# Performer features in two row halves of the array, two chunks of tokens at a time

## The chip, the cores and the metric

The program runs on one core of one Trainium2 chip. The metric is device time in microseconds (us), the median of several executions; one more execution is recorded by the hardware profiler. The engines are named as in the profile: PE is TensorE (matrix products), PEld its weight loads, DVE is VectorE, ACT is ScalarE, POOL is GpSimd, SP is SyncE.

## The reference

The model is a stack of four layers on an input of 8 images of 128 channels and 16 x 16 pixels (256 tokens an image, 2048 in all). Layer 0 is an "adder" convolution (sums of absolute differences), layer 1 a Mamba block, layer 2 attention and a mixture of experts, layer 3 a Performer with eight inner layers and a spectral filter at the end. The change is in the attention of the Performer: each head of 16 dimensions turns its keys and queries into 44 positive features.

```python
B, W, D, H, DEP, LAT = (8, 8192, 128, 8, 4, 10)
DH = D // H          # 16
M = 44
def softmax_kernel(data, proj, is_query, eps=0.0001):
    dn = data.shape[-1] ** (-0.25)
    ratio = proj.shape[0] ** (-0.5)
    dd = jnp.einsum('bhnd,md->bhnm', data * dn, proj)
    diag = jnp.sum(data * data, axis=-1, keepdims=True) * 0.5 * (dn * dn)
    if is_query:
        mx = jnp.max(dd, axis=-1, keepdims=True)
    else:
        mx = jnp.max(dd, axis=(-1, -2), keepdims=True)
    return ratio * (jnp.exp(dd - diag - mx) + eps)
...
    qp = softmax_kernel(q, proj[i], True)
    kp = softmax_kernel(k, proj[i], False)
    d_inv = 1.0 / jnp.einsum('bhnm,bhm->bhn', qp, jnp.sum(kp, axis=2))
    ctx = jnp.einsum('bhnm,bhnd->bhmd', kp, v)
    o = jnp.einsum('bhnm,bhmd->bhnd', qp, ctx) * d_inv[..., None]
...
for i in range(lo, lo + DEP):
    t = t + attn(layer_norm(t, ln1_g[i], ln1_b[i]), i)
    u = layer_norm(t, ln2_g[i], ln2_b[i])
    t = t + (jax.nn.gelu(u @ W1[i] + b1[i], approximate=False) @ W2[i] + b2[i])
```

## The kernel before

Everything is in fp32. Channels lie on the 128 partitions, tokens along the free dimension. The 2048 tokens are four blocks of 512 (`BLK`), each of two images.

**Two streams, two blocks each.** `_performer_stream` is a Python generator that writes the instructions of layers 2 and 3 for two blocks. There are two such streams. `interleave` takes one step (up to the next `yield True`) of each in turn, and `performer_layer` first runs 16 steps of stream 0 alone (`HALF_LAYER`), so that one stream is about half a Performer layer ahead: while one is in its feed-forward part (products `p`, GELU), the other is in its attention. Inside a stream the attention of its two blocks (`_performer_attention`, called with `j` = 0 and 1) advances in lockstep, a step of one and then a step of the other (L1351). The order of the steps gives each instruction a priority; a scheduler at compile time takes the ready instruction of the highest priority for each engine, and each engine then runs its queue in that fixed order.

**Buffers.** Each stream has four PSUM banks of 512 fp32 (`bank`, L1263), shared by both its blocks; every product goes to a fresh bank, and a bank is free again when its last reader is done. The exponentials `ex` of the queries have two buffers for each block, `ek` of the keys holds all four chunks.

**Attention of one block**, in steps:

- `rotated` makes `k` and `q`, [128 = 8 heads x 16 dimensions, 512 tokens]; then the squares' sums `dg` by two rounds of products into `pl`.
- Keys: the block's 512 tokens are four chunks `c` of 128. For each, one step: the product `pf` (L1464) has the chunk of `k` as weights (128 rows, 128 tokens) and `w["f"]` as the moving operand, [128, 352], a matrix of eight 16 x 44 blocks on the diagonal (line 175) and zeros elsewhere: all eight heads at once. DVE takes the maximum over each head's 44 features (L1466) and subtracts it (L1468); ACT takes the exponential (L1471).
- The key maxima over all tokens (`pm`, `pg`), the values `pv` and their factors `vo`.
- Queries: `query(c)` does the same with `pq` (L1508), a reduction (L1511), a small addition of 8 elements (L1512), a subtraction (L1514) and an exponential (L1515). Chunks 0 and 1 come in a step each, ahead of the sums over tokens `pc` (two steps).
- `turned(c, ex)`: four transposes of 128 tokens x 88 features (two heads) into one bank `px`, and an ACT pass (L1522) that adds a constant and writes `qp`. Four steps: `turned(0)` and `query(2)`, `turned(1)` and `query(3)`, `turned(2)`, `turned(3)`.
- `pn`: products of `qp` with `ctx`, numerators and denominators, in four groups of 32 columns of the array; then `po` (L1582) and the addition to `H`.

There are 8 layers x 4 blocks = 32 such attentions: 128 products `pf` and 128 `pq`. `S.mm` (L265 in the profile for every product) is one call of the language's matmul; in the profile it stands as two LDWEIGHTS and two MATMUL records. Transposes (L1521, L1479, L1449) are one each.

**Other names.** `pd` (L636) is a product of the Mamba layer with only 8 rows, `pg` (L1485) one of the Performer with 16 rows. `Tables.use` (L278) loads tables for ACT: one set holds Exp and Ln, another GELU, and a load stands wherever the order of ACT's work changes from one to the other.

Of the kernel before, what the change touches and what calls it, by code (L numbers as in the profile page):

```python
# [10 lines left out]
F32 = mybir.dt.float32  # L11
AF = mybir.ActivationFunctionType
ALU = mybir.AluOpType
AX = mybir.AxisListType
PSUM = bass.MemoryType.PSUM

P = 128
# [18 lines left out]
NH = 8  # L36
DH = 16
M = 44
HM = NH * M
PAIR = 2 * M  # L40
NPAIR = NH // 2
# [253 lines left out]
def bc(ap, axis, n):  # L295

    a = ap.unsqueeze(axis)
    shape = list(a.shape)
    shape[axis] = n
    return a.to_broadcast(shape)  # L300
# [561 lines left out]
class _Fuse:  # L862
# [23 lines left out]
    def bank(self, shape, name):  # L886
        return self.psum.tile(shape, F32, tag="f", name=name)
# [323 lines left out]
def performer_layer(E, W):  # L1211
# [3 lines left out]
    with ExitStack() as ctx:  # L1215
# [29 lines left out]
        with tc.high_priority(offset=tc.cur_priority - E.mark):  # L1245
            for _ in range(HALF_LAYER):
                next(streams[0])
# [3 lines left out]

EXCHANGE = [i ^ 1 for i in range(32)]

HALF_LAYER = 16


# [70 lines left out]
def _performer_stream(S, blocks):  # L1327
# [18 lines left out]
    for i in range(NL):  # L1346
        w = _layer(S, i)
        sums = [two.tile([P, 2], F32, tag=f"us{j}", name="us3") for j in range(2)]
        us = yield from _norms(S, h, S.v(f"ln1_g{i}"), S.v(f"ln1_b{i}"), sums)
        parts = [_performer_attention(S, i, w, h[j], us[j], sums[j], j) for j in range(2)]  # L1350
        while parts:  # L1351
            parts = [p for p in parts if next(p, None)]
# [49 lines left out]
def _performer_attention(S, i, w, H, u, sums, j):  # L1402
# [6 lines left out]
    nc, two, many = S.nc, S.two, S.many  # L1409
    ident = S.c("ident")  # L1410

    def rotated(name):
        pa = bank(S, [P, 2, L], "pa3")
        S.mm(pa.rearrange("p b l -> p (b l)"), w[name], u)
        bias = S.v(f"b{name}{i}")
        r = two.tile([P, 2, L], F32, tag="r" + name, name="r" + name)
        o = many.tile([P, 2, L], F32, tag="t", name="ro3")
        nc.vector.scalar_tensor_tensor(o, pa, bias, bc(S.c("sin"), 1, 2), ALU.add, ALU.mult)

        sq = many.tile([P, BLK], F32, tag="t", name="sq" + name)  # L1420
        nc.scalar.activation(sq, pa.rearrange("p b l -> p (b l)"), AF.Square, bias=bias)
        nc.vector.scalar_tensor_tensor(r, pa, bias, bc(S.c("cos"), 1, 2), ALU.add, ALU.mult)  # L1422
        o = o.rearrange("p b l -> p (b l)")
        nc.vector.stream_shuffle(o, o, EXCHANGE)
        r = r.rearrange("p b l -> p (b l)")
        nc.gpsimd.tensor_add(r, r, o)  # L1426
        return r, sq

    k, sqk = rotated("k")
    yield True  # L1430
    q, sqq = rotated("q")
# [18 lines left out]
    dg = two.tile([P, 4, 2, NH], F32, tag="dg", name="dg3")  # L1450
# [5 lines left out]
        nc.vector.tensor_scalar(ub[:, b, :], S.ones[:, 0:PAIR], sums[:, b : b + 1], KEPS, ALU.mult, ALU.mult)  # L1456


    mx = two.tile([P, 4, NH], F32, tag="mxk", name="mxk")
    ek = two.tile([P, 4, HM], F32, tag="ek", name="ek3")  # L1460
    for c in range(4):
        yield True
        pf = bank(S, [P, HM], "pf3")
        S.mm(pf, k[:, c * P : (c + 1) * P], w["f"])  # L1464
        f = pf.rearrange("p (h m) -> p h m", m=M)
        nc.vector.tensor_reduce(mx[:, c, :], f, AX.X, ALU.max)  # L1466
        e = ek[:, c, :]
        nc.vector.tensor_tensor(  # L1468
            e.rearrange("p (h m) -> p h m", m=M), f, bc(mx[:, c, :], 2, M), ALU.subtract
        )  # L1470
        nc.scalar.activation(e, e, AF.Exp, scale=0.5)  # L1471
    yield True

    m2 = two.tile([P, 2, NH], F32, tag="m2", name="m2")
# [29 lines left out]
    qp = two.tile([P, NPAIR, BLK], F32, tag="g", name="qp")[0:PAIR]  # L1504

    def query(c):
        pf = bank(S, [P, HM], "pq3")
        S.mm(pf, q[:, c * P : (c + 1) * P], w["f"])  # L1508
        f = pf.rearrange("p (h m) -> p h m", m=M)
        mq = two.tile([P, NH], F32, tag="mq", name="mq")  # L1510
        nc.vector.tensor_reduce(mq, f, AX.X, ALU.max)  # L1511
        nc.vector.tensor_tensor(mq, mq, dg[:, c, 1, :], ALU.add)  # L1512
        ex = two.tile([P, HM], F32, tag=f"ex{j}", name="ex")
        nc.vector.tensor_tensor(ex.rearrange("p (h m) -> p h m", m=M), f, bc(mq[:, :], 2, M), ALU.subtract)  # L1514
        nc.scalar.activation(ex, ex, AF.Exp, scale=0.5)  # L1515
        return ex

    def turned(c, ex):
        px = bank(S, [PAIR, NPAIR, P], "px3")
        for n in range(NPAIR):  # L1520
            nc.tensor.transpose(px[:, n, :], ex[:, n * PAIR : (n + 1) * PAIR], ident)  # L1521
        nc.scalar.activation(qp[:, :, c * P : (c + 1) * P], px, AF.Identity, bias=S.keps[0:PAIR, :])  # L1522

    ex = []
    for c in range(2):
        yield True
        ex.append(query(c))

    yield True

# [24 lines left out]
        bc(ks[:, :, :], 3, DH),  # L1555
        ALU.mult,
    )
    for c in range(4):
        yield True
        turned(c, ex[c])  # L1560
        if c + 2 < 4:
            ex.append(query(c + 2))

    yield True
    pn = [bank(S, [P, BLK], "pn3") for _ in range(2)]
# [201 lines left out]
```

## Time and profile before

| | |
|---|---|
| median of 3 executions | 3185.94 us (3185.02 to 3186.75) |
| the profiled execution | 3185.76 us |
| its span, first to last instruction | 3184.0 us |
| mean granted TensorE clock | 0.985 |
| PE busy, whole span | 2947.6 us (93%), 16686 MATMUL |
| DVE busy | 2437.6 us (77%) |
| ACT busy | 2204.9 us (69%) |
| POOL busy | 732.8 us (23%) |

The span falls into the adder layer (to about 1000 us), the Mamba layer (to about 1860 us), layer 2 (to about 2000 us), the Performer (to about 2900 us with both streams at work) and the end of the last stream with the spectral filter. "Busy" counts a matmul from its start to its modelled end, the last 0.17 us of which overlap the next one's start; a waiting engine is told by the "idle before" of the group it waits to run, with the releaser behind the arrow. Line numbers are those of the kernel before.

### The profile page before, as it was taken

The page shows a single profiled execution, that of the slowest core. Times are in us where ns is not written, and L with a number is a line of the kernel's source. Part 1 is how long each engine was busy: PE and PEld are TensorE (multiplying, and loading weights), DVE is VectorE, ACT ScalarE, POOL GpSimd, SP SyncE. Part 2 cuts the span into 40 slices and gives each one's busy share as a digit, 9 for nine tenths or more (in the row PEclk, how much of TensorE's full clock was granted, in tenths as well). Part 3 has the DMA queues.
Part 4 walks back from the last instruction along what each step waited for, and adds up shares of the span by engine and source line. Part 5 has one row for each costly group of instructions (what it writes and reads, how often), then busy time and mean ns, then how long its engine had stood idle before and what let it go on. Part 6 is the DMA issues. An engine that isn't in the chain of part 4 may idle for free.

```text
span 3184.0 us, 42472 instructions
## 1 busy us (share of the span) xinstructions
PE 2947.6 (93%) x16686; PEld 1299.8 (41%) x16686; DVE 2437.6 (77%) x3419; ACT 2204.9 (69%) x2653; POOL 732.8 (23%) x433
## 2 busy tenths in 40 slices
PE   6999999999997778998997988999999999999999
PEld 2333332333332223333433444555555555555444
DVE  6999999999996999999999257676576577574531
ACT  6999999999995887778776143666667766767111
POOL 3000000000001788778878000010010010010110
PEclk9999999999998999999999998999999999999999
DMA  1000000000001443443443000000000000001100
GB/s 38 1 1 5 1 1 5 1 1 5 1 1 47 166 147 127 146 142 127 151 141 125 17 27 13 1 13 1 13 13 1 13 13 1 13 1 37 53 27 14
DMA packets 39196, 131.47 MB, mean 41 GB/s; under 512 B 7490, under 2 KB 10572, under 8 KB 37588
## 3 DMA queue, kind: packets, MB, share of 16 engines
q1 hardware_dynamic: 38564, 128.02, 11.9%
q8 instruction: 132, 2.16, 0.3%
q10 hardware_dynamic: 432, 0.73, 0.1%
q14 instruction: 68, 0.56, 0.1%
HBM read 125.85 MB, written 1.84 MB: 40 GB/s over the span
## 4 chain that ended last, share of the span: by engine, by line
PE 65%; DVE 22%; ACT 6%; POOL 4%; issue 2%; DMA 1%; DVEq 0%; ACTq 0%; POOLq 0%; SPq 0%
PE o L265 30%; PE p L265 8%; DVE st L839 8%; DVE hc L848 4%; PE g L265 3%; PE pc L265 3%; PE conv L265 3%; PE acc L265 2%; PE pq L265 2%; PE xc L265 2%; PE var L265 2%; POOL dbu L753 2%; PE pv L265 1%; PE pn L265 1%; PE px L1521 1%
## 5 line engine op out<-in xcount | busy, mean ns | idle before, releaser
L265 PE MATMUL o<-d,sel 128*32 128x512 f32 x8800 | 946.4, 592 | 5.5 <-DVE d L432 5.5
L434 ACT ACTIVATE d<-sh,w 128x2048 f32<-128x2048 f32 x460 | 886.3, 1996 | 63.3 <-PE o L265 54.8
L432 DVE TENSOR_SCALAR d<-sh,w 128x2048 f32<-128x2048 f32 x640 | 789.4, 1291 | 47.5 <-PE o L265 39.8
L753 POOL TENSOR_TENSOR dbu<-du,bs 128x1024 f32<-128x1024 f32 x191 | 447.1, 2368 | 1019.4 <-DVE du L727 990.5
L265 PEld LDWEIGHTS o<-d,sel 128*32 128x32 f32 x8800 | 298.2, 110 | 653.0 <-issue 540.9
L839 DVE TENSOR_TENSOR_SCAN st<-da,dbu 128x512 f32<-128x512 f32 x384 | 447.9, 1207 | 13.3 <-POOL dbu L753 11.3
L265 PE MATMUL acc<-hc,cst 128*128 128x512 f32 x768 | 377.3, 616 | 84.8 <-DVE hc L848 84.3
L766 ACT ACTIVATE da<-delta,neg_a 128x510 f32<-128x510 f32 x384 | 256.6, 685 | 81.4 <-DVE st L839 80.4
L265 PEld LDWEIGHTS acc<-hc,cst 128*128 128x128 f32 x768 | 137.1, 192 | 293.4 <-DVE hc L848 173.1
L848 DVE TENSOR_TENSOR hc<-st,pcs 128x1024 f32<-128x1024 f32 x192 | 234.5, 1221 | 25.4 <-ACT tok L894 0.5
L1426 POOL TENSOR_TENSOR rk<-rk,ro 128x512 f32<-128x512 f32 x32 | 40.8, 1275 | 890.3 <-DVE rk L1422 620.5
L758 ACT COPY pcs<-cs 128x512 f32<-128x512 f32 x192 | 112.6, 586 | 79.9 <-DVE hc L848 78.5
L1699 ACT COPY ug<-p 128x512 f32<-128x512 f32 x64 | 37.5, 586 | 177.0 <-PE p L265 177.0
L265 PE MATMUL p<-u,lw 128*128 128x512 f32 x256 | 128.7, 621 | 15.2 <-DVE u L1321 13.3
L265 PE MATMUL conv<-pad,f 128*128 128x512 f32 x288 | 133.8, 598 | 3.2 <-ACT pad L994 2.1
L426 DVE SCALAR_TENSOR_TENSOR d<-sh,w,d 128x2048 f32<-128x2048 f32 x52 | 122.3, 2352 | 1.9
L265 PE MATMUL p<-T,H 128*128 128x512 f32 x256 | 115.6, 602 | 7.3 <-DVE ug L1701 6.3
L1471 ACT ACTIVATE ek<-ek 128x352 f32<-128x352 f32 x128 | 59.8, 492 | 88.0 <-DVE ek L1468 87.8
L1522 ACT ACTIVATE qp<-px,keps 88x512 f32<-88x512 f32 x128 | 84.2, 678 | 51.8 <-PE px L1521 51.2
L265 PE MATMUL p<-g,lw 128*128 128x512 f32 x256 | 114.6, 595 | 0.8 <-ACT g L1363 0.8
L265 PE MATMUL g<-ug,me 128*128 128x512 f32 (+1 forms) x320 | 112.0, 509 | 0.0
L1299 ACT ACTIVATE lsq<-xc 128x512 f32<-128x512 f32 x80 | 47.4, 596 | 76.3 <-PE xc L265 76.2
(322 smaller groups left out, 4064.0 us busy)
## 6 DMA issues: line engine op xcount, KB each, us to landing
bs<-rows SPq DMA_DIRECT2D x96, 512.0 KB, 3.9
cs<-rows SPq DMA_DIRECT2D x96, 512.0 KB, 4.8
m<-in_Mphi SPq DMA_DIRECT2D x8, 1024.0 KB, 4.9
lw<-in_layers SPq DMA_DIRECT2D x8, 948.0 KB, 4.6
f<-in_fuse SPq DMA_DIRECT2D x2, 1152.0 KB, 8.1
T<-in_T SPq DMA_DIRECT2D x1, 2064.0 KB, 8.1
x<-in_x SPq DMA_DIRECT2D x4, 256.0 KB, 6.2
total<-sums SPq DMA_DIRECT2D x16, 64.0 KB, 2.0
```

Source lines behind the costliest of these rows:

```text
L265: self.nc.tensor.matmul(out, lhsT=lhsT, rhs=rhs, start=start, stop=stop)
L426: nc.vector.scalar_tensor_tensor(held, tap(k), w[:, k, f : f + 1], held, ALU.max, ALU.add)
L432: nc.vector.tensor_scalar(d, tap(k), wk, None, ALU.max)
L434: nc.scalar.activation(d, tap(k), AF.Abs, scale=-1.0, bias=wk)
L753: gen.tensor_tensor(dbs[r], got[r // NST]["du"], bc(row("bs", r), 1, 2), ALU.mult)
L758: nc.scalar.copy(pcs[r], row("cs", r))
L766: nc.scalar.activation(das[g % 3][:, :, 1:], d[:, :, 1:], AF.Exp, scale=a)
L839: nc.vector.tensor_tensor_scan(st[:, h, :], da, dbs[r][:, h, :], 0.0, ALU.mult, ALU.add)
L848: nc.vector.tensor_tensor(hc, st, bc(pcs[r][:, :], 1, 2), ALU.mult)
L1299: nc.scalar.activation(sq, xc, AF.Square)
L1471: nc.scalar.activation(e, e, AF.Exp, scale=0.5)
L1522: nc.scalar.activation(qp[:, :, c * P : (c + 1) * P], px, AF.Identity, bias=S.keps[0:PAIR, :])
```

## The change

The keys and queries get one helper, `features(src, c, name)`. It takes two chunks of tokens, `c` and `c + 1`, and two banks. Heads 0 to 3 lie on partitions 0 to 63 and their features in the first 176 columns of `w["f"]`; heads 4 to 7 on partitions 64 to 127 and the last 176 columns. For each chunk `t` and half `r` there is one product with 64 rows, 128 tokens and 176 moving columns, into bank `r` at the place `t`. So a call makes four products of a quarter of the area in place of two full ones: the blocks of `w["f"]` that hold only zeros are left out. Bank `r` then holds 2 chunks x 4 heads x 44 features.

What reads the banks goes by halves of the heads in place of chunks: reduction, subtraction and exponential have the same number of elements (352 a partition) and are as many as before. `r = 0` is read in the step of the products, `r = 1` a step later. `turned(c, r, ex)` transposes two pairs of heads for two chunks (four transposes as before) and writes half of the heads of 256 tokens of `qp` in one ACT pass.

The steps: the keys still have four. The queries of chunks 0 and 1 still have two. The part after `pc` has five in place of four: `turned(0, 0)`; `turned(0, 1)` and the products and first half of chunks 2 and 3; their second half; `turned(2, 0)`; `turned(2, 1)`.

```diff
+HALF = P // 2
...
+    half = HM // 2
     mx = two.tile([P, 4, NH], F32, tag="mxk", name="mxk")
     ek = two.tile([P, 4, HM], F32, tag="ek", name="ek3")
-    for c in range(4):
+
+    def features(src, c, name):
+        pf = [bank(S, [P, 2, half], name) for _ in range(2)]
+        for t in range(2):
+            for r in range(2):
+                rows = slice(r * HALF, (r + 1) * HALF)
+                cols = slice((c + t) * P, (c + t + 1) * P)
+                S.mm(pf[r][:, t, :], src[rows, cols], w["f"][rows, r * half : (r + 1) * half])
+        return [p.rearrange("p t (h m) -> p t h m", m=M) for p in pf]
+
+    for c in (0, 2):
         yield True
-        pf = bank(S, [P, HM], "pf3")
-        S.mm(pf, k[:, c * P : (c + 1) * P], w["f"])
-        f = pf.rearrange("p (h m) -> p h m", m=M)
-        nc.vector.tensor_reduce(mx[:, c, :], f, AX.X, ALU.max)
-        e = ek[:, c, :]
-        nc.vector.tensor_tensor(
-            e.rearrange("p (h m) -> p h m", m=M), f, bc(mx[:, c, :], 2, M), ALU.subtract
-        )
-        nc.scalar.activation(e, e, AF.Exp, scale=0.5)
+        for r, f in enumerate(features(k, c, "pf3")):
+            m = mx[:, c : c + 2, r * NH // 2 : (r + 1) * NH // 2]
+            nc.vector.tensor_reduce(m, f, AX.X, ALU.max)
+            e = ek[:, c : c + 2, r * half : (r + 1) * half]
+            nc.vector.tensor_tensor(
+                e.rearrange("p t (h m) -> p t h m", m=M), f, bc(m, 3, M), ALU.subtract
+            )
+            nc.scalar.activation(e, e, AF.Exp, scale=0.5)
+            if r == 0:
+                yield True
...
     def query(c):
-        pf = bank(S, [P, HM], "pq3")
-        S.mm(pf, q[:, c * P : (c + 1) * P], w["f"])
...
+        out = []
+        for r, f in enumerate(features(q, c, "pq3")):
+            heads = slice(r * NH // 2, (r + 1) * NH // 2)
+            mq = two.tile([P, 2, NH // 2], F32, tag=f"mq{r}", name="mq")
+            nc.vector.tensor_reduce(mq, f, AX.X, ALU.max)
+            nc.vector.tensor_tensor(mq, mq, dg[:, c : c + 2, 1, heads], ALU.add)
+            ex = two.tile([P, 2, half], F32, tag=f"ex{j}", name="ex")
+            nc.vector.tensor_tensor(ex.rearrange("p t (h m) -> p t h m", m=M), f, bc(mq[:, :, :], 3, M), ALU.subtract)
+            nc.scalar.activation(ex, ex, AF.Exp, scale=0.5)
+            out.append(ex)
+            if r == 0:
+                yield True
+        return out
+
+    def turned(c, r, ex):
+        px = bank(S, [PAIR, 2, 2 * P], "px3")
+        for n in range(2):
+            for t in range(2):
+                nc.tensor.transpose(px[:, n, t * P : (t + 1) * P], ex[:, t, n * PAIR : (n + 1) * PAIR], ident)
+        nc.scalar.activation(
+            qp[:, 2 * r : 2 * r + 2, c * P : (c + 2) * P], px, AF.Identity, bias=S.keps[0:PAIR, :]
+        )
+
+    yield True
+    ex = yield from query(0)
...
-    for c in range(4):
-        yield True
-        turned(c, ex[c])
-        if c + 2 < 4:
-            ex.append(query(c + 2))
+    for c in (0, 2):
+        for r in range(2):
+            yield True
+            turned(c, r, ex[r])
+        if c == 0:
+            ex = yield from query(2)
```

More of the change, by code (lines that the diff above doesn't have):

```diff
@@ L1506, in query @@
     def query(c):
-        pf = bank(S, [P, HM], "pq3")
-        S.mm(pf, q[:, c * P : (c + 1) * P], w["f"])
[L1509 to L1525, printed above, removed]
-        yield True
-        ex.append(query(c))
+        out = []
[21 more added lines that the diff above has]
+    ex = yield from query(0)
     yield True
@@ L1557, in _performer_attention @@
     )
-    for c in range(4):
-        yield True
-        turned(c, ex[c])
-        if c + 2 < 4:
-            ex.append(query(c + 2))
+    for c in (0, 2):
[4 more added lines that the diff above has]
+            ex = yield from query(2)
     yield True
```

## The prediction

> **What bounds the kernel now.** I read the granted clock first (0.985, nothing disturbed), then the slices of the span: the Performer fills most of slices 25 to 36, where TensorE (PE) is at 9 tenths and VectorE (DVE) and ScalarE (ACT) at 5 to 7. Then the busy times of 1990 to 2900 us, seven and a half of the eight layers:
>
> ```profile
> core 0: us, PE busy (x) PEld busy (x) DVE busy (x) ACT busy (x) POOL busy (x), PEclk, DMA share, GB/s
> 1990.00:2900.00 910.00, 864.79 (x4877) 494.80 (x4878) 599.48 (x1570) 610.27 (x980) 76.83 (x60) 0.98 0.02 7
> ```
>
> PE is busy 864.79 of 910 us (95%), DVE and ACT two thirds. Next, the groups of that window that the diff touches, and the chain of waits inside it:
>
> ```profile
> L265 PE MATMUL pq<-lw,rq 128*128 128x352 f32 x250 | 89.2, 465 | 0.0
> L265 PE MATMUL pf<-lw,rk 128*128 128x352 f32 x240 | 81.1, 462 | 0.1
> L1511 DVE TENSOR_REDUCE mq<-pq 128x8 f32<-128x352 f32 x125 | 64.0, 518 | 41.5 <-PE pq L265 41.5
> L1466 DVE TENSOR_REDUCE mxk<-pf 128x8 f32<-128x352 f32 x120 | 59.8, 516 | 11.4 <-PE pf L265 10.3
> ...
> by line: PE p L265 20.4%; PE pc L265 10.3%; PE pq L265 7.4%; PE xc L265 4.8%; PE pv L265 4.4%; PE var L265 3.7%; PE px L1521 3.2%; PE pn L265 3.2%; DVE mxk L1466 2.8%; DVE ek L1468 2.5%; issue 2.3%; PE pf L265 2.1%; ACT qp L1522 2.0%; DVE r
> ```
>
> PE never idles before pq, and DVE waits 41.5 us for it but only 10.3 us for pf. On the chain pq has 7.4% (67 us), pf 2.1% (19 us).
>
> **The price of a product.** One product in the code is two MATMUL records (whole trace: pf x256 for 128 products): fp32 goes in two passes. A 512-wide pass reads 592 ns, a 352-wide one 459 at best; the difference over 160 columns is 0.83 ns a column, which leaves a tail of 166 ns that overlaps the next. Passes follow each other at 0.83 ns x width + 2 ns: 0.295 us for 352 columns, 0.149 for 176. On the chain, pq carries 67 of 250 x 0.295 = 74 us (0.91) and pf 19 of 71 (0.27); I use these two shares to turn PE time into time of the end.
>
> **What the change removes and adds.** It handles two chunks per call, 64 calls for keys and 64 for queries.
>
> 1. *Passes.* Two chunks cost 4 x 0.295 = 1.18 us now. After: 8 passes of 64 rows and 176 columns. No row of this trace has two halves of the rows at work. Nearest are products in four groups of 32 columns:
>
> ```profile
> 2313.24 0.42 PE L265 MATMUL pl<-sqk,cst 128*32 128x128 f32 x8
> 2313.49 0.83 PE L265 MATMUL pn<-qp,ctx 88*32 88x256 f32 x12
> ```
>
> Eight 128-wide passes end to end would take 8 x 0.109 + 0.166 = 1.04 us; they took 0.42, two slots and the tail. So four tiles ran at once, both passes of each. If the row halves do as well, a call takes 4 x 0.149 = 0.60 us; if not at all, 8 x 0.149 = 1.19. I take 0.60: same instruction, same engine, only the other axis. Gain 0.585 us a call.
>
> *The page "TensorE: Matmul & The Clock Gate" of the Trainium skill, Part 3 "What overlaps and what doesn't", has matmuls start and end in strict program order. With the two passes of a product behind each other, a call would then need five slots, 0.745 us, and some 0.149 x 64 x (0.91 + 0.27) = 11 us of the gain would go. The eight pl passes in 0.42 us speak against it: in strict order they need five slots and the tail, 0.70.*
>
> 2. *The change of tiles.* Today almost all products use the whole array. The array changes to few rows at pd (8 rows), pg (16 rows):
>
> ```profile
> 1172.51 0.19 PEld L265 LDWEIGHTS acc<-hc,cst 128*128 128x128 f32 x1 [0.24 <-issue]
> 1173.45 0.29 PEld L265 LDWEIGHTS pd<-proj,w_dtproj 8*128 8x128 f32 x2 [0.76 <-ACT da L766]
> ...
> L265 PE MATMUL pd<-proj,w_dtproj x48: 587/588/692, 1012.5 to 1673.2; 8*128 8x512 f32 x48
> ```
>
> In a plain stream weights load one pass ahead, every 0.43 us. The load for pd should have come at 1172.94 and came at 1173.45, when the earlier passes had run out (about 1173.36), and pd's first pass is 692 ns in place of 588: its 105 ns of load lie bare. With each pass's stream taken as start to end less 166 ns, the gap into few rows is 0.196 us (median of 39 in the whole trace, lowest 0.194, so it is no data wait), and back 0.200 (61). A call that stands alone pays 0.396 us, two in a row share it. In the trace pf's 128 products stand in 56 unbroken runs, pq's in 89. Bounds: 32 runs for 64 calls (the two blocks always together) and 64 (never); splitting each call gives 128. I take 48: at the first call of each kind all banks are open to both blocks; at the second they come free one by one.
>
> *"TensorEngine Tiling (Array Packing)" in the Trainium skill, Key Properties, says that a change of tiling mode drains the engine. It gives no figure; a sum that leaves the drain out would forecast some 22 us more gain than mine. The pd rows agree that there is a drain.*
>
> Keys and queries each: 64 x 0.585 - 48 x 0.396 = 18.4 us of PE. On the path 18.4 x 0.91 = 17 for queries and 18.4 x 0.27 = 5 for keys: 22 us. With 32 runs 29, with 64 runs 14, with 128 runs a loss of 16.
>
> 3. *DVE and ACT.* Reduce, subtract and exp stay as many and as long (352 elements, 518, 515 and 492 ns): the two chunks of half the heads take the place of one chunk of all. One more level in a pattern is free: L1496 with three levels 687 ns, L1580 flat 685 for the same 512 elements. The add at L1512 (162 ns) stays, 8 elements. Transposes and their evacuation (678 ns) keep number and size. 0, bounds -1 and +2 us.
>
> 4. *Banks.* A stream has four, for both blocks. Now each product takes one. After, a call takes two, and r = 1 is read a step later. At the second query call the queue of PE holds two px and two calls, six banks. The second block's call waits for one px to be evacuated (678 ns) and one half to be read (518 + 162 + 518 = 1.20 us). PE is in order, so everything behind it waits too: the other stream's products, then DVE for those. What covers it is the other stream's work that the scheduler puts first; without cover up to 64 x 1.2 = 77 us, below 0 nothing. Before pq the idle column reads 0.0, so I take a tenth: 7 us.
>
> 5. *One more yield a layer* (the second query call spans two steps). It issues nothing, but stream 0 meets stream 1 elsewhere. By counting steps, the four GELU steps of each stream still meet as many steps with Exp (four and three), so the table loads (1283 ns each, 123 in this window) should stay. One pair more per layer and stream would be 41 us of ACT, mostly in its idle third. I take 0, bounds -8 and +10 us. No DMA is issued, dropped or passed; SP's and POOL's queues keep their order.
>
> Sum: 22 - 7 = 15 us less. The profiled execution took 3185.76 us, its span 3184.0, against a median of 3185.94, so the sum goes on the median: **3171 us**. Without the bank term 3164.
>
> **The rivals.**
> - *Banks in pairs (slower).* The mechanism of point 4, at the second calls. From 22 / 64 = 0.34 us of bare wait per second call it eats the gain. At half of the 1.2 us it costs 38 us: 3186 + 16 = 3202. For: DVE already waits 41.5 us for pq, at the very place. Against: two streams, and PE with other work ready.
> - *The halves don't overlap (the change doesn't do what it says).* Then a call is 1.19 + 48/64 x 0.396 = 1.49 in place of 1.18 us: 64 x 0.31 x (0.91 + 0.27) = 23 us, and the banks' 7: 3216. Against: pl and pn above; for: nothing in the trace shows rows.
> - *Nothing on the path.* The keys' features are set by DVE (1.03 us a chunk against 0.59 of PE), and at pq the DVE and ACT behind them take over: 3186, give or take 7. Against: 95% of PE.
>
> **How the numbers follow.** Forecast (3148 to 3179) 0.53; banks 0.20; no overlap 0.09; nothing on the path 0.18. A difference under 0.2% (6.4 us, about what these runs can tell from none) is "same". The last case is same with 0.12, faster and slower with 0.03 each. So faster 0.56, same 0.12, slower 0.32. The range goes down to 3148 (all calls paired, no bank wait, the keys carried further: 29 us and the bound of point 5) and up to 3210 over the bank case; below lie 0.06, above the no-overlap case and a rest of the banks, 0.13.
>
> **What would show it.** Passes of pf and pq as x512 each of 64*128, 176 wide, best 313 ns (146 + 166), a lone call in 0.8 us with its tail against 1.35 for two products now. Streams of eight with gaps of 0.2 us on both sides, in about 96 runs. PE busy in this stage down by some 35 us; DVE's idle time before mq down from 41.5 if the forecast holds, up if the banks decide. The reductions at 515 to 520 ns, 123 table loads in the stage. The prediction is wrong if a call takes over 1 us between its gaps, if the calls are torn into more than 128 runs, or if PE idles before pq for more than 20 us.

## The result and the profile after

The changed kernel takes 3200.24 us (median of 5, 3197.12 to 3204.69) against 3186.75 us for the kernel before on the same chip (median of 5): a ratio of 1.0044 with a 95% interval of 1.003 to 1.0059. It is slower by 13.5 us; 15 us faster had been forecast. The profiled execution took 3197.12 us, its span 3195.3.

The busy times of the Performer's stage, in the columns of the view shown of the kernel before:

```profile
1990.00:2900.00 910.00, 858.32 (x5333) 490.31 (x5333) 598.53 (x1567) 587.59 (x963) 76.44 (x60) 0.99 0.02 8
```

PE is busy 858 in place of 865 us of the 910, so nearly as full, although the features' passes should have taken some 35 us less. The groups of the same window show the passes themselves; the idle time in front of each and its releaser stand behind the last bar:

```profile
L265 PE MATMUL pq<-lw,rq 64*128 64x176 f32 x496 | 70.5, 340 | 0.0
L265 PE MATMUL pf<-lw,rk 64*128 64x176 f32 x480 | 64.0, 332 | 7.8 <-DVE ek L1481 7.8
L265 PE MATMUL p<-u,lw 128*128 128x512 f32 x240 | 119.5, 617 | 25.3 <-ACT ek L1484 14.3 <-DVE u L1323 7.8 <-ACT g L1365 3.3
L1526 DVE TENSOR_REDUCE mq<-pq 128x8 f32<-128x352 f32 x124 | 61.4, 518 | 21.4 <-PE pq L265 20.7
L1479 DVE TENSOR_REDUCE mxk<-pf 128x8 f32<-128x352 f32 x120 | 59.5, 517 | 10.0 <-PE pf L265 9.2
```

DVE's instructions are as long as before (517, 518 ns) and DVE waits less for pq than it did (20.7 against 41.5 us). So the readers did not pay. PE waits 7.8 us for DVE ahead of pf, which it did not do before: that is the wait for a bank. Its longest idle time in the stage lies ahead of p, the feed-forward's first product: 25.3 us, where the kernel before had 15.2. The chain of the window:

```profile
by line: PE p L265 19.4%; PE pc L265 10.1%; PE xc L265 7.2%; PE pq L265 7.2%; PE pa L265 5.8%; PE var L265 5.4%; PE pf L265 4.4%; PE pn L265 4.3%; PE pv L265 3.9%; PE px L1540 3.8%; PE po L265 3.5%; ACT lsq L1309 1.7%; DVE u L1315 1.6%; DVE
```

pq keeps its share (7.2% after 7.4%) and pf doubles its own (4.4% after 2.1%). The order of PE's matmuls shows why:

```profile
2193.20 0.60 PE L1540 MATMUL px<-cst,ex 128*88 128x128 f32 x4
2193.73 0.87 PE L265 MATMUL pq<-lw,rq 64*128 64x176 f32 x8
2194.53 0.64 PE L1540 MATMUL px<-cst,ex 128*88 128x128 f32 x4
2195.10 0.86 PE L265 MATMUL pq<-lw,rq 64*128 64x176 f32 x4
2195.89 1.12 PE L265 MATMUL pa<-u,lw 128*128 128x512 f32 x2
2196.94 0.86 PE L265 MATMUL pq<-lw,rq 64*128 64x176 f32 x4
```

The line of x8 is a whole call: eight passes in 0.87 us, which is 0.107 of bare weight load, four slots of 0.149 and the tail of 0.166. The two lines of x4 are one call torn in two. Each holds both chunks of one half of the rows, with a product of the other stream (pa) between them. Each takes 0.86 us, as much as a whole call, because its four passes use the same half and run one behind the other; and each has a change of tiles on both sides.

In the order that the compiler fixes for PE the 512 products stand in 136 runs: of these 33 are one whole call and 16 two whole calls, 48 hold only products of one half (23 of half 0, 25 of half 1), and the rest are pieces of three or one, some joined to a neighbour. Counting the longer half of each run, the passes need 327 slots of two passes where 256 would do. In the trace some pass streams during 102 us (pf 50 and pq 52, the union of the passes' times without their tails and bare weight loads); 76 had been forecast, and the kernel before needs 151. The gaps around the calls are as forecast: 0.196 us into the row halves (median of 136), 0.200 back.

### The profile page after: what moved, and what is told of

It reads as the page before. It is cut to its first block, busy times and chain, and to the rows that moved or that the text cites. A ratio compares the mean times of both kernels' runs of the same rounds, so it can differ in the third digit from the quotient of the medians.

```text
span 3195.3 us, 43401 instructions
## 1 busy us (share of the span) xinstructions
PE 2954.9 (92%) x17198; PEld 1304.0 (41%) x17198; DVE 2440.4 (76%) x3419; ACT 2187.8 (68%) x2641; POOL 733.7 (23%) x433
## 4 chain that ended last, share of the span: by engine, by line
PE 68%; DVE 21%; ACT 5%; POOL 4%; issue 2%; DMA 1%; DVEq 0%; ACTq 0%; POOLq 0%
PE o L265 30%; DVE st L839 9%; PE p L265 8%; DVE hc L848 5%; PE g L265 3%; PE pc L265 3%; PE xc L265 3%; PE pq L265 2%; PE var L265 2%; PE pa L265 2%; PE conv L265 2%; PE acc L265 2%; POOL dbu L753 1%; PE po L265 1%; PE pf L265 1%
## 5 line engine op out<-in xcount | busy, mean ns | idle before, releaser
L265 PE MATMUL p<-u,lw 128*128 128x512 f32 x256 | 126.6, 615 | 25.3 <-ACT ek L1484 14.3
L1373 DVE SCALAR_TENSOR_TENSOR H<-p,vecs,H 128x512 f32<-128x512 f32 x32 | 24.0, 751 | 112.4 <-PE p L265 112.4
```

Source lines behind the costliest of these rows:

```text
L265: self.nc.tensor.matmul(out, lhsT=lhsT, rhs=rhs, start=start, stop=stop)
```

## The experiments

Each ran on one chip beside the kernel before, mostly five times or more. The kernels before read 3183.8 to 3186.8 us there, so a difference between two runs can be off by some 3 us where they stood beside different ones. "Full rows" means that each of the four products of a call takes all 128 rows and the same 176 columns: the zero blocks are multiplied, and everything else stays.

**Full rows in the changed kernel.**

```diff
-                S.mm(pf[r][:, t, :], src[rows, cols], w["f"][rows, r * half : (r + 1) * half])
+                S.mm(pf[r][:, t, :], src[:, cols], w["f"][:, r * half : (r + 1) * half])
```

> The changed kernel, but each of its products takes all 128 rows (with the zero blocks of the features' matrix): same banks, same steps, same readers, no change of tiles and no overlap. Theory A (the array pays: torn calls and 136 changes of tiles each way): PE work as in the kernel before, so 3183 to 3191 us, and no idle gap of 0.2 us around the features. Theory B (banks taken in pairs and read a step later): the loss stays, 3197 to 3206 us.

Measured: 3171.64 us, ratio 0.9963 (0.995 to 0.9975), below what either theory gave. The order of every queue is the same as in the changed kernel, instruction by instruction, so the two differ in nothing but the rows: row halves cost 28.6 us (26.5 when each is taken against the kernel before beside it). Banks in pairs, half the heads at a time and the later step cost nothing here; with full rows they gain 13 us. Theory B falls. The same place of the order, with full rows:

```profile
2182.98 1.36 PE L265 MATMUL pq<-lw,rq 128*128 128x176 f32 x8
2184.18 0.60 PE L1540 MATMUL px<-cst,ex 128*88 128x128 f32 x4
2184.61 0.76 PE L265 MATMUL pq<-lw,rq 128*128 128x176 f32 x4
2185.21 1.02 PE L265 MATMUL pa<-u,lw 128*128 128x512 f32 x2
2186.07 0.76 PE L265 MATMUL pq<-lw,rq 128*128 128x176 f32 x4
```

A whole call takes longer (1.36 against 0.87 us), a torn half less (0.76 against 0.86), and the next product starts 0.60 us after a torn half's start, against 0.79 in the row halves (2184.61 to 2185.21; 2195.10 to 2195.89). With the gap in front of it, 0.99 against 0.60 us a torn half. Setting the two traces side by side at each of the 136 runs, from the end of the matmul before to the start of the one behind (tails left out, bare weight loads counted as gaps): 187.8 against 173.6 us. So 14.2 of the 28.6 us lie at the calls themselves: 27.3 us more ahead of them, 44.1 less within, 30.9 more behind.

**The four products of a call in a fixed order.**

```diff
-            for r in range(2):
+            for r in (1, 0):
...
+                if last is not None:
+                    behind(S, ins, last)
+                last = ins
```

(`behind` tells the scheduler to put one instruction after another, without a wait on the chip.)

> The changed kernel with its four products of a call put in the fixed order half 1, half 0, half 1, half 0, so that the compile-time order cannot put both chunks of one half ahead of the other half. In the fixed order of PE the runs stay at 135 (136 before) and the slots that the passes need fall from 327 to 289 of 0.298 us, 11 us of PE. Theory A: 5 to 11 us faster than the changed kernel, 3189 to 3196. Theory B: the call now waits for its second bank before the rest goes on, 3200 to 3212.

Measured: 3198.1 us, 1.0037 (1.0023 to 1.0051). Some 2 us better than the changed kernel, within the spread: the passes stream during 91 us in place of 102, but 22 times the first product alone goes ahead of the others, and the runs stay 135. The time lies between the two expectations and tells neither theory from the other.

**New form for the keys alone, and for the queries alone**, each the changed kernel with the other part as before:

> The new form for the keys alone, queries as before. 62 runs with 0.396 us of change of tiles each (24.6 us) against 75.5 - 48 = 27.5 us of passes saved: PE work 3 us less. Theory A: the queries make the loss, 3183 to 3192. Theory B: the keys' banks are read a step later as well, 3190 to 3198, half of the loss.

> The new form for the queries alone (with the extra step), keys as before. 74 runs (29.3 us) against 75.5 - 48.3 = 27.2 us saved: PE work 2 us more. Theory A: on the chain the queries weigh three times the keys, so most of the loss is here or in the waits behind torn calls: 3190 to 3200. Theory B: the six banks wanted at the second call decide, 3194 to 3204, more than the keys alone.

Measured: keys 3188.51, 1.0011 (1.0002 to 1.002); queries 3192.28, 1.0021 (1.0011 to 1.0032). Each is a little slower than before and the two together (0.32%) make most of the 0.44%; both lie in theory A's ranges and below theory B's. What each consists of was open until their twins with full rows ran:

> The twin of the run with the new form for the keys alone: full rows, the same order of every queue. The whole change costs 28.6 us more in row halves than in full rows (3200.24 against 3171.64). Measured at the calls, in the order of the whole change, the keys took 12.7 us of the 14.3 us that row halves cost there, the queries 1.6. If the price arises where the calls stand: 3172 to 3181 here (row halves 3188.5), the larger part. If it is spread over both by waits and the clock: 3180 to 3189.

> The twin of the run with the new form for the queries alone. If the price arises where the calls stand: 3188 to 3192 here (row halves 3192.3), next to no difference. If it is spread over both by waits and the clock: 3174 to 3184. The lower of the two twins also says which half of the regrouping makes the gain of 13 us with full rows.

Measured: keys 3175.1, 0.9967 (0.9955 to 0.9979); queries 3185.06, 0.9997 (0.9989 to 1.0006). So row halves cost 13.4 us at the keys and 7.2 at the queries; together that is 20.6 of the 28.6 us, the rest comes only with both. Most of the gain of the regrouping is the keys' (9.7 of 13 us). The keys came out where the price arises at the calls, the queries between their two expectations, and neither place is free.

**One more step in the kernel before.**

```diff
         if c + 2 < 4:
             ex.append(query(c + 2))
+        if c == 1:
+            yield True
```

> The kernel before with the one more step after turned(1) and query(3), nothing else. Asks where the 13 us come from by which the changed kernel with full rows beat the kernel before. If from the place where the two streams meet: 3168 to 3177 us. If from the regrouping (two chunks in two banks, another order of the queues, 119 loads of ACT tables in place of 131; here they stay 131): 3181 to 3191.

Measured: 3186.33, 1.0008 (0.9999 to 1.0016): no gain. It is the regrouping, not the step.

**One product of the four in 64 rows.**

```diff
-                S.mm(pf[r][:, t, :], src[rows, cols], w["f"][rows, r * half : (r + 1) * half])
+                part = rows if t == r == 0 else slice(0, P)
+                S.mm(pf[r][:, t, :], src[part, cols], w["f"][part, r * half : (r + 1) * half])
```

> The changed kernel in which only the first of the four products of a call takes 64 rows, the other three all 128: every call makes one change of tiles each way (128 runs), and nothing overlaps. PE gets 128 x 0.396 = 51 us more than with full rows (3172 us). Theory A (a change of tiles costs the end what it costs PE, less cover): 3202 to 3228. Theory C (other waits cover it and the torn calls are the loss): 3172 to 3188.

Measured: 3213.15, 1.0094 (1.008 to 1.0108): 41.5 us more than full rows, for 51 us of PE. Theory A holds for the changes of tiles: about four fifths of their price reaches the end. The order of every queue is again that of full rows, and the trace has the 128 changes into 64 rows (0.197 us) and back (0.201) that were expected.

**The second half read in the same step, products chained; row halves and full rows.**

```diff
             nc.scalar.activation(e, e, AF.Exp, scale=0.5)
-            if r == 0:
-                yield True
+        yield True
```

(and the same in `query`)

> Row halves in a kinder order: the second half of a call is read in the same step as the first (the yield stands behind both), and the four products are chained as in the run before. 116 runs and 282 slots: 46 + 84 = 130 us of PE for the features against 153 with full rows in the same order (the twin run beside it). Theory A (slots and changes of tiles are the whole price): 10 to 23 us faster than the twin. Theory D (a further price, the clock of the array or waits behind the calls, which the sum lacks): from 5 us faster to 15 us slower than the twin.

> The twin: the same program with all 128 rows in each product; the order of every engine's queue is the same, instruction by instruction. No change of tiles and no overlap for the features. 101 loads of ACT tables in place of 119: 3155 to 3175 us, the fastest so far if the order of ACT's work is what gains.

Measured: row halves 3185.37, 1.0007 (0.9998 to 1.0016); full rows 3186.88, 1.001 (1.0001 to 1.0019). The twins are level where slots and changes of tiles promised 22.6 us: theory D. In the traces the row halves save only 7.5 us at the calls, counted at full clock, and 7.7 us more at half clock takes that back (the table below). The forecast for full rows fell too: 101 table loads, the fewest of all, and no gain, so the number of table loads does not decide.

**Calls that can't be torn; row halves and full rows.**

```diff
         pf = [bank(S, [P, 2, half], name) for _ in range(2)]
+        marks = [nc.vector.memset(p[:, 0, 0:1], 0.0).ins for p in pf]
...
+                if last is not None:
+                    behind(S, ins, last)
+                else:
+                    for mark in marks:
+                        behind(S, ins, mark)
+                last = ins
```

(the chain of the four products starts with half 0 here)

> Row halves that are never torn: DVE first writes one element into each of a call's two banks, and the first product waits for both writes, so that no product starts before the call has both banks. The order of PE has 89 runs, all of whole calls (50 alone, 39 in twos), and 256 slots: 76 + 35 = 112 us for the features against 153 with full rows. Theory A (tearing is what made the change slower; untorn calls gain): 15 to 40 us faster than its twin with full rows, and below 3184. Theory D (what the calls save turns into waits and a lower clock elsewhere): within 10 us of the twin.

> The twin of the run with the marks: all 128 rows in each product, the same order of every queue. Against the changed kernel with full rows (3172 us) it adds 256 small writes of DVE (some 60 to 160 ns each, 15 to 41 us of DVE) and the waits of PE for them: 3172 to 3200 us.

Measured: row halves 3199.22, 1.0044 (1.0032 to 1.0057); full rows 3210.81, 1.0081 (1.0067 to 1.0094). Now no call is torn (89 runs, all whole), and row halves are 11.6 us faster than full rows: the sign turns. Theory A's sign, but less than its size, and just outside theory D's 10 us. The marks and the order that they force cost 39 us (3210.81 against 3171.64), more than the 28 that had been allowed, so neither is below 3184. At the calls the row halves save 34.1 us (163.6 against 197.7). The stage of both, row halves first:

```profile
1990.00:2900.00 910.00, 833.78 (x5282) 476.70 (x5282) 601.02 (x1800) 582.90 (x958) 76.20 (x60) 0.98 0.02 7
```

```profile
1990.00:2900.00 910.00, 854.48 (x5236) 536.03 (x5235) 595.62 (x1779) 573.84 (x944) 76.30 (x60) 0.99 0.02 7
```

PE is busy 20.7 us less in the same time, and little more work is done in it (46 records of 5236): part of what the calls save is idled away. The largest part of the added idle time lies ahead of p (24.6 against 15.7 us), row halves first again:

```profile
L265 PE MATMUL p<-u,lw 128*128 128x512 f32 x240 | 126.5, 647 | 24.6 <-ACT ek L1499 18.7 <-DVE u L1328 5.9
```

```profile
L265 PE MATMUL p<-u,lw 128*128 128x512 f32 x236 | 116.5, 614 | 15.7 <-ACT ek L1499 14.6
```

And the granted clock falls.

**Where the rest is: the clock.** In the changed kernel one such place, in stretches of 3.4 us (columns as above, the clock in front of the last two):

```profile
2207.40:2210.80 3.40, 2.81 (x41) 1.54 (x35) 3.40 (x10) 1.71 (x4) 1.78 (x2) 1.00 0.00 0
2210.80:2214.20 3.40, 2.00 (x16) 1.46 (x14) 3.40 (x9) 0.50 (x1) 0.76 (x1) 1.00 0.00 0
2214.20:2217.60 3.40, 3.40 (x6) 1.17 (x5) 1.83 (x4) 0.50 (x1) 0.00 (x0) 0.51 0.00 0
2217.60:2221.00 3.40, 3.40 (x6) 1.00 (x4) 2.47 (x6) 0.77 (x2) 0.00 (x0) 0.50 0.00 0
```

and its matmuls:

```profile
2210.07 1.56 PE L265 MATMUL pf<-lw,rk 64*128 64x176 f32 x16
2212.93 0.83 PE L265 MATMUL pf<-lw,rk 64*128 64x176 f32 x4 [1.30 <-DVE ek L1481]
2213.87 1.73 PE L265 MATMUL po<-rd,lw 128*128 128x512 f32 x2
2215.53 0.95 PE L265 MATMUL pf<-lw,rk 64*128 64x176 f32 x2
2216.41 2.07 PE L265 MATMUL po<-rd,lw 128*128 128x512 f32 x2
```

Two blocks' calls go through in 1.56 us and hold all four banks; PE then idles 1.30 us until DVE has read one (ek L1481). PE was busy 2.00 of 3.40 us, and for the next 6.8 us the clock is at one half: the 512-wide po takes 2.07 us for a product that needed 1.13 elsewhere in the kernel before. Here the products ran ahead of a slower reader, PE stood idle, and half clock followed. But such a hole alone does not decide it. At the same place about one layer later the two calls take 1.55 us and PE then idles 1.31 us for the same reader. It was busy for still less, 1.81 of 3.41 us, and the clock stayed full:

```profile
2330.30:2333.71 3.41, 1.81 (x17) 1.42 (x17) 3.41 (x11) 0.33 (x2) 2.07 (x2) 1.00 0.00 0
2333.71:2337.13 3.42, 3.26 (x10) 1.67 (x11) 3.15 (x6) 0.93 (x2) 0.00 (x0) 1.00 0.02 5
```

What else the clock goes by isn't shown.

What half clock costs can be read from the traces. PE has the same matmuls in the same order in both kernels of a pair, so two traces can be set side by side matmul by matmul, from the first call to the last. The difference (row halves less full rows, counted from each start to the next) is sorted into three parts: where either of the two was at half clock; the rest at the calls, up to the start of the second matmul behind each run; and all other work at full clock. One profiled execution of each, in us:

| form | time at half clock, row halves | full rows | calls, full clock | other work, full clock | at half clock | sum | difference of the medians |
|---|---|---|---|---|---|---|---|
| the whole change | 37.8 | 8.3 | +8.9 | -1.2 | +14.1 | +21.8 | +28.6 |
| keys alone | 38.2 | 24.2 | +1.7 | +2.3 | +7.0 | +11.0 | +13.4 |
| queries alone | 44.6 | 25.3 | +1.8 | -0.1 | +8.8 | +10.5 | +7.2 |
| read in one step, chained | 36.2 | 20.6 | -7.5 | -1.5 | +7.7 | -1.3 | -1.5 |
| never torn | 41.0 | 27.3 | -25.9 | +8.3 | +3.0 | -14.5 | -11.6 |

In all five pairs the row halves spend 14 to 30 us more at half clock, and 3 to 14 us of the difference lie there, no more than half of the added time. In the whole change the calls cost 8.9 us at full clock, half clock 14.1, and other work nothing. (The 14.2 us at the calls above hold some 6 us at half clock.) Outside the calls, plain waiting weighs more than half clock only where they are never torn.

The whole traces are 27.4 us apart; the 5.6 us that the sum lacks lie before the first call and behind the last. The clock is not one trace's chance: the mean granted clock was 0.980 to 0.983 in the five executions of the changed kernel and 0.986 to 0.990 with full rows, 0.981 to 0.983 and 0.986 to 0.987 where the calls are never torn, 0.983 to 0.986 and 0.987 to 0.989 with the read in one step. (For keys or queries alone the ranges touch.) Still, the clock could not be held fixed, so the table is an account of one trace each and not an experiment.

## Why the prediction was wrong, step by step

- **The step that failed** is "I take 48" in the second point, together with the first point's 0.60 us for every one of the 128 calls. Both took it that a call goes through in one piece. It gave 96 runs and 76 us of passes; the order has 136 runs and the trace 102 us. At 0.396 us a run that is 54 + 102 = 156 us for the features, against 151 before: 5 us more PE where 37 less were forecast. The bound with torn calls stood in the text (128 runs for each kind, a loss of 16) and was taken for remote; more than 128 runs was one of its own signs of being wrong.
- **A term that was missing** is the clock. The prediction read 0.985 as undisturbed and had no price for a change in it; in the traces 14.1 us of the difference to full rows lie where the clock was at half.
- **Why calls tear** was in the fourth point: each call wants two of four banks. It was priced as a bare wait on the chip. But the scheduler knows of the missing bank too: by the order that it made, it puts the products whose bank is free first, then other work, then the rest. With both banks asked for ahead (the marks) not one call is torn. The rival "banks in pairs" (3202 us) had the cause, but not the mechanism: PE idles 0.0 us ahead of pq after the change. That its time came so near is luck.
- **The 7 us for banks** were placed at pq, where PE idles 0.0 us. The wait is at pf instead, 7.8 us with row halves and 2.4 with full rows. On balance the regrouping is no loss: with full rows the same banks, steps and order are 13 us faster than before.
- **The shares 0.91 and 0.27** of the chain, used to turn PE time into time of the end, failed for gains. Never torn, 34 us saved at the calls became 11.6, a third; the extra changes of tiles came through at four fifths. A chain says what is late now; after a saving something else is late instead (here what PE awaits ahead of p, 8.9 us more), and the clock changes with it.
- **Right**: the overlap of a whole call (0.87 us with load and tail), the two gaps of 0.196 and 0.200 us, DVE and ACT unchanged, the extra step (1.0008, not told from 1). The table loads were expected to stay and fell from 131 to 119, without visible effect. "The halves don't overlap" is refuted by the x8 in 0.87 us; "nothing on the path" by the 28.6 us between two programs that differ in rows alone, and by the 41.5 us of the added changes of tiles.

The version to keep is the changed kernel with full rows: 3171.64 us, ratio 0.9963 to the kernel before. Why the regrouping of the keys gains is not settled; that it has no time at half clock between 2000 and 2900 us, where the kernel before has 23.9 us, fits but is one trace.

## What to carry to other kernels

A tiled array pays only for products that stay together: count the runs in the compiled order, not the calls in the source, and charge each run for both changes of tiles (0.4 us here, against 0.6 us that a whole call of eight passes saved). If the tiles need several buffers at once, a scheduler that hands buffers out one by one can tear them apart; if the first product is to ask for all of them, price that too (39 us here). Look at the granted clock of both kernels before you put a difference down to the work. And try the regrouping without the tiling: here the part that looked like a cost was the gain.

## What the runs showed of the hardware

- Two halves of the rows do run at once in fp32, both passes of each: in the trace of the changed kernel the two halves' first passes start 6 to 7 ns apart, although in the program the whole product of one half is one instruction ahead of the other's, and eight passes take four slots (0.87 us with load and tail). Their weight loads overlap as well (two loads of 128 columns for 64 rows, 6 to 7 ns apart).
- Going into and out of 64-row tiles costs the same 0.196 and 0.200 us as the 8- and 16-row products did before.
- Half clock comes in stretches of 3.41 us or a multiple of it. One stretch in which PE was busy for 2.00 of 3.40 us was followed by 6.8 us at half clock, another with 1.81 of 3.41 us by full clock, with nearly the same idle stretch in both (1.30 and 1.31 us). The page "TensorE: Matmul & The Clock Gate" of the Trainium skill, Part 1, has the clock fall back after one idle window of about 3.4 us. The length agrees; but the clock fell here after a window that was 59% busy, so "idle" is too strict, and the busy share alone doesn't tell which window it is.
- At half clock a 512-wide product took 2.07 us in place of 1.13.
